# Expert rows added to the output by accumulating scatters instead of being stored and gathered

## The chip, the cores and the metric

The kernel runs on one core of a Trainium2 chip. The metric is the device time of one execution in microseconds. Three timed runs of the kernel before gave 521.59, 524.7 and 526.0 us, a median of 524.7 us. The execution that the profiler recorded took 525.11 us, and its span, from the first to the last instruction, is 523.0 us.

## The reference, cut to what matters

The program is one layer of a graph network: 625 nodes with 512 features, a two-layer relational graph convolution and a linear-attention block side by side, and then a feed-forward block with routed experts. Only the last block is touched. It computes, for each node row (the capacity never binds for 625 nodes):

```python
f = _layernorm(x)
y = gelu(f @ Ws1 + bs1) @ Ws2 + bs2                 # shared expert
for bank in ("sp", "fq"):                           # two banks of 8 experts
    probs = softmax(f @ Wr + br)
    expert = argmax(probs)                          # one expert a node and bank
    gate = probs[expert]
    h = gelu(f @ W1[expert] + b1[expert])           # 512 -> 128
    y += gate * (h @ W2[expert] + b2[expert])       # 128 -> 512
out = x + y
```

Each node takes one expert in each of two banks, so each output row is the node's residual row plus one shared term and two gated expert rows. With the inputs of this case the reference sends 1, 0, 226, 17, 321, 60, 0 and 0 nodes to the experts of the first bank, and 0, 0, 6, 31, 306, 20, 130 and 132 to those of the second.

## The kernel before, in words

Nodes are tiled as 5 blocks of 125 rows (`NT`, `TP`). A tile scheduler fixes each engine's order of instructions when the program is built, from the order in the source and from priorities. Where two tiles share a tag they share memory, and the later one waits until the earlier one is no longer read.

The end of the kernel, from line 1240 on, goes so:

- **Residual and normalised rows.** `x1` holds the residual of every node in SBUF, `fn` its layer norm. `fn` is stored to DRAM (`fn_d`, line 1245).
- **Routing.** VectorE (DVE) finds each node's expert in each bank, its place in the order sorted by expert (`place`), and the list of nodes in that order (`node_i`, lines 1284 to 1321).
- **Windows.** Each expert's nodes are cut into windows of 128 rows (`WIN`). `NW` = 12 windows a bank are always computed, since up to 12 can be needed. `offs` holds for every window the offset of its expert's weights and its first row (lines 1324 to 1350); TensorE and DVE load these as registers. `slot_i` says for each node in which of the 12 x 128 window rows its result stands (line 1360).
- **Shared expert.** Line 1382 computes it, with the gated expert biases (`mT`, `b2x`), two products a block, and line 1383 adds it to `x1` on DVE.
- **Sorted rows.** GpSimd (POOL) gathers `fn` rows in sorted order by indirect transfers (line 1400, 5 a bank), TensorE turns them (line 1408), and ACT and DVE copy them into `sortT`.
- **First expert layer**, a loop over the 12 windows (lines 1412 to 1419): DVE copies the window's weights to `stage1`, TensorE does 4 products, ACT applies Gelu into `hid`.
- **Second expert layer**, another loop over the 12 windows (lines 1420 to 1424): one product, a copy out of PSUM into one of 4 buffers of `stage` by ACT, or in the first bank by ACT and DVE in turn, and a store of 128 rows to DRAM (`back_d`) from SyncE's queue (SP).
- **Rows back to their nodes** (lines 1425 to 1433): for each block POOL gathers 125 rows of `back_d` by `slot_i`, DVE multiplies them by `gate` and adds them to `x1`, and after the second bank SP stores the block of the output. The gathers' buffer of the first bank has tag A, which is also the tag of `sort_fq`, the second bank's sorted rows.

The two banks go one after another on TensorE. PSUM buffers for the second layer (`narrow`) are two.

Of the kernel before, what the change touches and what calls it, by code (L numbers as in the profile page):

```python
# [40 lines left out]
EARLY = 2  # L41
WIN = 128
NW = (N + NX * (WIN - 1)) // WIN
WHOLE = 1.5 * 2 ** 23


# [542 lines left out]
def tile_fast(ctx: ExitStack, tc: tile.TileContext, a: dict, out: bass.AP, flag):  # L589
# [10 lines left out]
    def fourth(tag, name, shape=(TP, NT, H)):  # L600
        return main.tile(list(shape), F32, tag=tag, name=name)
# [167 lines left out]
    def nodes(t):  # L769
        return slice(t * TP, (t + 1) * TP)  # L770
# [426 lines left out]
    nc.gpsimd.tensor_copy(low_2, lower)  # L1197
    number = const.tile([TP, NT], F16, name="number")
    nc.gpsimd.iota(number, pattern=[[TP, NT]], base=0, channel_multiplier=1, allow_small_or_imprecise_dtypes=True)
    iota_w = const.tile([128, NW], F32, name="iota_w")  # L1200
    nc.gpsimd.iota(iota_w, pattern=[[1, NW]], base=0, channel_multiplier=0, allow_small_or_imprecise_dtypes=True)

# [67 lines left out]
        return ap[:, :, None].to_broadcast([TP, G, NX])  # L1270

    SW = KC * N + WIN
    room = main.tile([128, 2 * NT * H], F32, tag="U", name="room")
    sortT = [room[:, :SW], main.tile([128, SW], F32, tag="A", name="sort_fq")]
    halves = room[:TP, SW:].bitcast(F16)
# [121 lines left out]
    back_d = [dram.tile([NW * WIN, H], F32, name=f"back{i}") for i in range(2)]  # L1397
# [5 lines left out]
    for i in range(2):  # L1403
        sT = sortT[i][:, :KC * N].rearrange("p (k n) -> p k n", n=N)
        for t in range(NT):
            ps = wide_ps("ps_sT")[:, :KC * 128].rearrange("p (k n) -> p k n", n=128)
            for k in range(KC):
                nc.tensor.transpose(ps[:, k, :TP], rows_s[i][:, t, k * 128:(k + 1) * 128], ident[:TP, :TP])
            (nc.vector.tensor_copy if t % 2 else nc.scalar.copy)(sT[:, :, nodes(t)], ps[:, :, :TP])
        at = offsets(i, 0, (NX - 1) * H, [mybir.EngineType.PE, mybir.EngineType.DVE])  # L1410
        start = offsets(i, 1, N - 1, [mybir.EngineType.PE])
        for w in range(NW):
            w1s = stage1[:, w % 4, :]
            nc.vector.tensor_copy(w1s, we1[i][:, bass.ds(at[w], KC * FF)])
            ps = wide_ps("ps_hid")[:, :WIN]
            for k in range(KC):
                nc.tensor.matmul(ps, w1s[:, k * FF:(k + 1) * FF], sortT[i][:, k * N:][:, bass.ds(start[w], WIN)],
                                 start=(k == 0), stop=(k == KC - 1))
            nc.scalar.activation(hid[i][:, w * WIN:(w + 1) * WIN], ps, AF.Gelu, bias=bias[:, i, w:w + 1])
        for w in range(NW):  # L1420
            ps = narrow([(hid[i][:, w * WIN:(w + 1) * WIN], we2[i][:, bass.ds(at[w], H)])], m=WIN)
            y = stage[:, w % 4, :]
            (nc.vector.tensor_copy if w % 2 and not i else nc.scalar.copy)(y, ps)
            nc.sync.dma_start(back_d[i][w * WIN:(w + 1) * WIN, :], y)
        yg = fourth("AX"[i], f"got{i}")
        for t in range(NT):
            nc.gpsimd.indirect_dma_start(  # L1427
                yg[:, t, :], None, back_d[i][:, :],
                bass.IndirectOffsetOnAxis(ap=slot_i[:, 2 * t + i:2 * t + i + 1], axis=0))
            nc.vector.scalar_tensor_tensor(x1[:, t, :], yg[:, t, :], gate[:, 2 * t + i:2 * t + i + 1], x1[:, t, :],  # L1430
                                           op0=ALU.mult, op1=ALU.add)
            if i == 1:
                nc.sync.dma_start(out[nodes(t), :], x1[:, t, :])


@with_exitstack
# [42 lines left out]
```

## Time and profile before

| what | value |
|---|---|
| median of the runs shown | 524.7 us |
| profiled execution | 525.11 us |
| its span | 523.0 us |
| mean granted TensorE clock | 0.938 |
| PE, DVE, ACT, POOL busy share | 87%, 71%, 39%, 16% |
| first gather of sorted rows starts | 418.74 us |
| first expert layer, bank sp, starts | 437.94 us |
| second expert layer, bank sp, starts | 448.76 us |
| first expert layer, bank fq, starts | 464.81 us |
| second expert layer, bank fq, starts | 477.22 us |
| last product of all | 492.45 us |
| last vector instruction of all | 511.17 us |

The shares of busy time cover the whole span, and in the first 400 us TensorE is busy nearly throughout. The change lies in the last 100 us, so that the stretches of that part, and not the shares, are what is to be read. The profile names a transfer by what it writes and reads (`back<-stage`), and a bracket at the end of a timeline line gives the engine's idle time before it and what ended that idle time.

### The profile page before, as it was taken

How to read it: one execution, taken by the hardware profiler on the slowest of the kernel's cores; microseconds unless marked ns; L12 is line 12 of the kernel's file. 1: busy time of each engine (PE TensorE's matmuls, PEld its weight loads, DVE VectorE, ACT ScalarE, POOL GpSimd, SP SyncE). 2: the span in 40 equal slices, each digit the busy share in tenths (PEclk: the TensorE clock that was granted, in tenths of full speed). 3: DMA queues.
4: the chain of work that ended last, by engine and by line, in shares of the span. 5: the costliest groups of instructions: out<-in, count | busy, mean ns of one | idle time of the engine just before them, and what ended most of it. 6: DMA issues, size and time to landing. Idle time of an engine off the chain costs nothing. (4 is left out here: it accounts for less than half of the span.)

```text
span 523.0 us, 5583 instructions
## 1 busy us (share of the span) xinstructions
PE 456.6 (87%) x1945; PEld 278.9 (53%) x1945; DVE 369.1 (71%) x452; ACT 202.7 (39%) x339; POOL 83.6 (16%) x117
## 2 busy tenths in 40 slices
PE   0389999999999999999999999999998799989400
PEld 0255358677665545687444769644444556566100
DVE  2659979999989769999999889997313454241220
ACT  1653149998998553161000345200001412334300
POOL 5700000000002111000000001970001071003140
PEclk9999999999999689999999889999999869989955
DMA  8957785453446957985767954995501542322742
GB/s 210 376 161 245 245 276 192 127 196 102 141 142 213 260 155 230 313 295 161 226 228 245 326 161 127 301 319 140 191 28 25 176 124 74 141 102 74 268 108 93
DMA packets 55751, 98.31 MB, mean 188 GB/s; under 512 B 6006, under 2 KB 14322, under 8 KB 55716
## 3 DMA queue, kind: packets, MB, share of 16 engines
q1 hardware_dynamic: 47204, 80.25, 47.4%
q0 software_dynamic: 8512, 17.63, 11.9%
q8 instruction: 18, 0.29, 0.2%
q14 instruction: 17, 0.14, 0.1%
HBM read 89.00 MB, written 8.85 MB: 187 GB/s over the span
## 5 line engine op out<-in xcount | busy, mean ns | idle before, releaser
L822 DVE SCALAR_TENSOR_TENSOR wrel<-basis_sb,att,wrel 128x2048 f32<-128x2048 f32 x107 | 246.0, 2346 | 7.7 <-DMA basis_sb<-in_L_gnn_basis_dram 5.7
L964 ACT ACTIVATE side<-iota_h,ed_f 125x630 f16<-125x630 f16 x96 | 71.9, 814 | 2.0 <-PE ps_cnt L969 2.0
L969 PE MATMUL ps_cnt<-side,oh_source 125*125 125x315 f16 x192 | 39.3, 302 | 0.2 <-DVE oh_source L966 0.2
L969 PEld LDWEIGHTS <-oh_source 125*125 125x125 f16 x192 | 25.7, 138 | 23.5 <-issue 15.4
L1220 PE MATMUL ps_acc<-wrel,agg 128*125 128x512 f32 x80 | 36.5, 596 | 0.3 <-DVE v L1240 0.3
L766 PE MATMUL ps_narrow<-wrel,agg 128*125 128x512 f32 x80 | 35.0, 592 | 0.0
L966 DVE TENSOR_SCALAR oh_source<-iota_h,col_m,ed_f 125x128 f16<-125x128 f16 x96 | 25.1, 312 | 10.9 <-PE ps_cnt L969 10.8
L1430 DVE SCALAR_TENSOR_TENSOR v<-got,work,v 125x512 f32<-125x512 f32 x10 | 7.5, 752 | 30.1 <-DMA got<-back,slot_i 30.1
L1089 PE MATMUL ps_agg<-cnt,high 125*128 125x314 f32 x160 | 26.9, 311 | 1.1 <-ACT wrel L854 1.1
L1089 PE MATMUL ps_agg<-cnt,low 125*128 125x314 f32 x160 | 26.4, 308 | 0.0
L1089 PEld LDWEIGHTS ps_agg<-cnt,high 125*128 125x128 f32 x160 | 24.1, 189 | 2.5 <-ACT wrel L854 2.0
L766 PEld LDWEIGHTS ps_narrow<-wrel,agg 128*125 128x125 f32 x80 | 15.0, 188 | 18.8 <-issue 18.8
L1089 PEld LDWEIGHTS ps_agg<-cnt,low 125*128 125x128 f32 x160 | 24.0, 189 | 0.8 <-issue 0.8
L1220 PEld LDWEIGHTS ps_acc<-wrel,agg 128*125 128x125 f32 x80 | 14.6, 187 | 17.5 <-issue 16.5
L766 PE MATMUL ps_narrow<-root,xnT 128*125 128x512 f32 x40 | 23.8, 739 | 0.0
L1183 POOL TENSOR_SCALAR_AFFINE_SELECT work<-work 125x125 f16<-125x125 f16 x1 | 23.7, 23719 | 0.0
L1240 DVE TENSOR_TENSOR v<-v,ps_acc 125x512 f32<-125x512 f32 x5 | 3.4, 687 | 26.7 <-PE ps_acc L1220 26.7
L1427 POOL DMA_INDIRECT got<-back,slot_i x10 | 12.1, 1211 | 59.7 <-PE ps_narrow L766 44.5
L760 PE MATMUL ps_wide<-zT,wq 128*128 128x512 f32 (+1 forms) x64 | 20.7, 433 | 0.0
L1105 ACT ACTIVATE gpre<-ps_narrow 125x512 f32<-125x512 f32 x5 | 3.0, 597 | 45.3 <-PE ps_narrow L766 45.3
L1220 PE MATMUL ps_acc<-root,gT 128*125 128x512 f32 x40 | 20.5, 647 | 0.0
L713 ACT COPY agg<-ps_agg 128x628 f32<-128x628 f32 x16 | 10.8, 680 | 22.9 <-PE ps_agg L1089 22.9
(282 smaller groups left out, 730.2 us busy)
## 6 DMA issues: line engine op xcount, KB each, us to landing
basis_sb<-in_L_gnn_basis_dram SPq DMA_DIRECT2D x56, 1024.0 KB
back<-stage SPq DMA_DIRECT2D x24, 256.0 KB
quad<-in_L_gnn_basis_dram POOLq DMA_DIRECT2D x16, 256.0 KB, 6.9
w<-in_L_mix_W_dram POOLq DMA_DIRECT2D x2, 1024.0 KB
root<-in_L_gnn_root_dram POOLq DMA_DIRECT2D x2, 1024.0 KB, 7.9
we_sp<-in_L_ffn_W_sp_dram SPq DMA_DIRECT2D x4, 512.0 KB
we_fq<-in_L_ffn_W_fq_dram SPq DMA_DIRECT2D x4, 512.0 KB
we_sp<-in_L_ffn_W_sp_dram SPq DMA_DIRECT2D x2, 1024.0 KB
```

Source lines behind the costliest of these rows:

```text
L713: nc.scalar.copy(dst, src)
L760: nc.tensor.matmul(ps[:, lo:hi], s, m[:, lo:hi], start=(i == 0), stop=(i == len(pairs) - 1))
L766: nc.tensor.matmul(ps[:m, :n], s, mv, start=(i == 0), stop=(i == len(pairs) - 1))
L822: final = nc.vector.scalar_tensor_tensor(dst, src, s, dst, op0=ALU.mult, op1=ALU.add)
L964: later(lambda: nc.scalar.activation(side, iota_h[:EP], AF.Sign, bias=row_f[:, c:c + 1]))
L966: later(lambda: nc.vector.tensor_scalar(os, iota_h[:EP, :128], col_m[:, m, c:c + 1], code_f[:, c:c + 1], op0=ALU.is_equal, op1=ALU.mult))
L969: nc.tensor.matmul(ps[:TP, s, :SEG + 1], os[:, :TP], side[:, s * SEG:(s + 1) * SEG + 1], start=(c == STEPS[m][0]), stop=(c == STEPS[m][-1]))
L1089: nc.tensor.matmul(ps[:, s, :SEG], y, cnt[:, r, m, s * SEG:(s + 1) * SEG].bitcast(F32R), start=(i == 0), stop=(i == len(pairs) - 1))
L1183: nc.gpsimd.affine_select(before, before, compare_op=ALU.is_ge, fill=0.0, base=-1, pattern=[[1, TP]], channel_multiplier=-1)
L1220: nc.tensor.matmul(accs[t], s, mv, start=start and i == 0, stop=stop and i == len(pairs) - 1)
L1427: nc.gpsimd.indirect_dma_start(yg[:, t, :], None, back_d[i][:, :], bass.IndirectOffsetOnAxis(ap=slot_i[:, 2 * t + i:2 * t + i + 1], axis=0))
L1430: nc.vector.scalar_tensor_tensor(x1[:, t, :], yg[:, t, :], gate[:, 2 * t + i:2 * t + i + 1], x1[:, t, :], op0=ALU.mult, op1=ALU.add)
```

## The change

The result of a window is no longer stored to a scratch tensor and gathered back. Instead:

- the output is first stored without the experts, block by block, right after line 1383;
- each window's result is multiplied by its rows' gates while it is copied out of PSUM into `stage` (ACT for even windows, DVE for odd ones, in both banks);
- POOL then issues an indirect transfer per window that adds the 128 rows of `stage` to the rows of the output in DRAM named by a list, `node_s`; a list entry of a row that holds no node lies beyond the last row, and is left out by the bounds check. Within a bank the scatters are declared independent of one another;
- the lists and gates in window order (`node_s`, `gate_s`) are made by products with one-hot matrices: ten of 125 x 128 against 125 x 24, for which DVE makes the one-hot rows and copies out the results;
- the loops of the two expert layers are merged: the second layer of window w follows the first layer of window w + 2 (`LAG`).

Stores to `back_d` (24), gathers from it (10) and the additions of gathered rows (10) go away; 24 scatters come in. The number of output stores stays at 5.

```diff
+LAG = 2
@@
-    slot_i = const.tile([TP, G], I32, name="slot_i")
...
-    nc.vector.tensor_tensor(slot_i, place, slot, op=ALU.subtract)
+    nc.vector.tensor_tensor(slot, place, slot, op=ALU.subtract)
+    window = small_tile(TP, G)
+    nc.vector.tensor_scalar(window, slot, 1.0 / WIN, (0.5 - WIN / 2) / WIN, op0=ALU.mult, op1=ALU.add)
+    nc.vector.tensor_scalar(window, window, WHOLE, -WHOLE, op0=ALU.add, op1=ALU.add)
+    nc.vector.scalar_tensor_tensor(slot, window, -float(WIN), slot, op0=ALU.mult, op1=ALU.add)
@@
+    both = spare[:TP, :4 * NT * NW].rearrange("p (j t i w) -> p j t i w", j=2, t=NT, i=2)
+    eq = both[:, 1]
+    nc.vector.tensor_tensor(eq, iota_w[:TP, None, None, :].to_broadcast([TP, NT, 2, NW]),
+                            window.rearrange("p (t i) -> p t i", i=2)[:, :, :, None].to_broadcast([TP, NT, 2, NW]),
+                            op=ALU.is_equal)
+    nc.vector.tensor_tensor(both[:, 0], eq, number1[:, :, None, None].to_broadcast([TP, NT, 2, NW]), op=ALU.mult)
+    nc.vector.tensor_tensor(eq, eq, gate.rearrange("p (t i) -> p t i", i=2)[:, :, :, None]
+                            .to_broadcast([TP, NT, 2, NW]), op=ALU.mult)
+    gate_s = small_tile(WIN, 2, NW)
+    node_s = const.tile([WIN, 2, NW], I32, name="node_s")
+    for i in range(2):
+        ps = pn.tile([128, 512], F32, tag="narrow", name="ps_rows")
+        ps = ps[:, :2 * NW].rearrange("p (j w) -> p j w", j=2)
+        for t in range(NT):
+            oh = spare[:TP, 4 * NT * NW + (t % 2) * WIN:4 * NT * NW + (t % 2 + 1) * WIN]
+            nc.vector.tensor_scalar(oh, iota_r[:TP], slot[:, 2 * t + i:2 * t + i + 1], None, op0=ALU.is_equal)
+            nc.tensor.matmul(ps, oh, both[:, :, t, i, :], start=(t == 0), stop=(t == NT - 1))
+        nc.vector.tensor_copy(gate_s[:, i, :], ps[:, 1, :])
+        none = small_tile(WIN, NW)
+        nc.vector.tensor_scalar(none, ps[:, 0, :], 0.0, 2.0 * N, op0=ALU.is_equal, op1=ALU.mult)
+        nc.vector.scalar_tensor_tensor(node_s[:, i, :], ps[:, 0, :], -1.0, none, op0=ALU.add, op1=ALU.add)
@@
         nc.vector.tensor_tensor(x1[:, t, :], x1[:, t, :], ps, op=ALU.add)
+        nc.sync.dma_start(out[nodes(t), :], x1[:, t, :])
@@
-        for w in range(NW):
-            w1s = stage1[:, w % 4, :]
...
-        for w in range(NW):
-            ps = narrow([(hid[i][:, w * WIN:(w + 1) * WIN], we2[i][:, bass.ds(at[w], H)])], m=WIN)
-            y = stage[:, w % 4, :]
-            (nc.vector.tensor_copy if w % 2 and not i else nc.scalar.copy)(y, ps)
-            nc.sync.dma_start(back_d[i][w * WIN:(w + 1) * WIN, :], y)
-        yg = fourth("AX"[i], f"got{i}")
-        for t in range(NT):
-            nc.gpsimd.indirect_dma_start(
-                yg[:, t, :], None, back_d[i][:, :],
-                bass.IndirectOffsetOnAxis(ap=slot_i[:, 2 * t + i:2 * t + i + 1], axis=0))
-            nc.vector.scalar_tensor_tensor(x1[:, t, :], yg[:, t, :], gate[:, 2 * t + i:2 * t + i + 1], x1[:, t, :],
-                                           op0=ALU.mult, op1=ALU.add)
-            if i == 1:
-                nc.sync.dma_start(out[nodes(t), :], x1[:, t, :])
+        added = []
+        def second(w):
+            ps = narrow([(hid[i][:, w * WIN:(w + 1) * WIN], we2[i][:, bass.ds(at[w], H)])], m=WIN)
+            y = stage[:, w % 4, :]
+            s = gate_s[:, i, w:w + 1]
+            if w % 2:
+                nc.vector.tensor_scalar(y, ps, s, None, op0=ALU.mult)
+            else:
+                nc.scalar.activation(y, ps, AF.Copy, scale=s)
+            add = nc.gpsimd.indirect_dma_start(
+                out[:, :], bass.IndirectOffsetOnAxis(ap=node_s[:, i, w:w + 1], axis=0), y, None,
+                bounds_check=N - 1, oob_is_err=False, compute_op=ALU.add)
+            if added:
+                tc.declare_no_dep(add.ins, group=f"rows{i}", reason="each node has one row in a bank's windows")
+            tc.add_to_no_dep_group(f"rows{i}", add.ins)
+            added.append(w)
+        for w in range(NW + LAG):
+            if w < NW:
+                w1s = stage1[:, w % 4, :]
...
+            if w >= LAG:
+                second(w - LAG)
```

More of the change, by code (lines that the diff above doesn't have):

```diff
@@ L1199, in tile_fast @@
     nc.gpsimd.iota(number, pattern=[[TP, NT]], base=0, channel_multiplier=1, allow_small_or_imprecise_dtypes=True)
+    number1 = const.tile([TP, NT], F32, name="number1")
+    nc.gpsimd.iota(number1, pattern=[[TP, NT]], base=1, channel_multiplier=1, allow_small_or_imprecise_dtypes=True)
+    iota_r = small_tile(128, WIN)
+    nc.gpsimd.iota(iota_r, pattern=[[1, WIN]], base=0, channel_multiplier=0, allow_small_or_imprecise_dtypes=True)
     iota_w = const.tile([128, NW], F32, name="iota_w")
@@ L1272, in tile_fast @@
     SW = KC * N + WIN
-    room = main.tile([128, 2 * NT * H], F32, tag="U", name="room")
+    room = main.tile([128, 2 * NT * H + 16], F32, tag="U", name="room")
+    spare = room[:, SW + (6 * N + 258) // 2:]
     sortT = [room[:, :SW], main.tile([128, SW], F32, tag="A", name="sort_fq")]
-    halves = room[:TP, SW:].bitcast(F16)
+    halves = room[:TP, SW:SW + (6 * N + 258) // 2].bitcast(F16)
     iota_n = halves[:, :N]
@@ L1395, in offsets @@
             skip_runtime_bounds_check_because="capped when they are made")[1]
-    back_d = [dram.tile([NW * WIN, H], F32, name=f"back{i}") for i in range(2)]
     for i in range(2):
@@ L1411, in tile_fast @@
         start = offsets(i, 1, N - 1, [mybir.EngineType.PE])
-        for w in range(NW):
-            w1s = stage1[:, w % 4, :]
[L1414 to L1419, printed above, removed]
@@ new lines, in tile_fast @@
+        for w in range(NW + LAG):
+            if w < NW:
+                w1s = stage1[:, w % 4, :]
+                nc.vector.tensor_copy(w1s, we1[i][:, bass.ds(at[w], KC * FF)])
+                ps = wide_ps("ps_hid")[:, :WIN]
+                for k in range(KC):
+                    nc.tensor.matmul(ps, w1s[:, k * FF:(k + 1) * FF], sortT[i][:, k * N:][:, bass.ds(start[w], WIN)],
+                                     start=(k == 0), stop=(k == KC - 1))
+                nc.scalar.activation(hid[i][:, w * WIN:(w + 1) * WIN], ps, AF.Gelu, bias=bias[:, i, w:w + 1])
+            if w >= LAG:
+                second(w - LAG)
```

## The prediction

> **What bounds the kernel now.** I read first the chain that ended last, since the change lies at the end; it reaches back only to 502.58 us, so I then read the timeline of the last 100 us, and the transfers in short stretches.
>
> In the timeline, POOL's first gather of window results starts at 478.33 us, as the second bank's first layer leaves its sorted rows. Its second set starts only when the last window is stored, at 498.39 us. From there nothing runs but five gathers, five additions and five stores:
>
> ```profile
> 477.22 6.43 PE L766 MATMUL ps_narrow<-we_fq 128*128 x14
> ...
> 478.33 1.21 POOL L1427 DMA_INDIRECT got<-back,slot_i  x1 [44.50 <-PE ps_narrow L766]
> ...
> 485.46 0.75 DVE L1430 SCALAR_TENSOR_TENSOR v<-got,work,v 125x512 f32<-125x512 f32 x1 [11.18 <-DMA got<-back,slot_i]
> ...
> 493.61 0.59 ACT L1423 COPY stage<-ps_narrow 128x512 f32<-128x512 f32 x1 [0.59 <-PE ps_narrow L766]
> 498.39 1.21 POOL L1427 DMA_INDIRECT got<-back,slot_i  x1 [12.80 <-DMA back<-stage]
> ...
> 504.46 1.21 POOL L1427 DMA_INDIRECT got<-back,slot_i  x1 [0.30 <-issue]
> 504.65 0.75 DVE L1430 SCALAR_TENSOR_TENSOR v<-got,work,v 125x512 f32<-125x512 f32 x1 [12.67 <-DMA got<-back,slot_i]
> 505.43 6.78 SPq L1433 DMA_DIRECT2D out_dram<-v  x5
> ...
> 511.17 0.75 DVE L1430 SCALAR_TENSOR_TENSOR v<-got,work,v 125x512 f32<-125x512 f32 x1 [1.53 <-DMA got<-back,slot_i]
> ```
>
> The columns of the next view are stretch, length, busy time of PE, PEld, DVE, ACT and POOL, granted clock, share of the 16 DMA engines, GB/s:
>
> ```profile
> 508.50:518.50 10.00, 0.00 (x0) 0.00 (x0) 1.50 (x2) 0.00 (x0) 0.00 (x0) 0.50 0.33 127
> 518.50:520.50 2.00, 0.00 (x0) 0.00 (x0) 0.00 (x0) 0.00 (x0) 0.00 (x0) 0.50 0.18 72
> 520.50:523.00 2.50, 0.00 (x0) 0.00 (x0) 0.00 (x0) 0.00 (x0) 0.00 (x0) 0.50 0.00 0
> ```
>
> The five output stores (1.28 MB) run at 127 GB/s, a third of the engines, until about 520; then 2.5 us of ending. So for the 29 us after the last product, which ends at 493.6, all computing engines are nearly idle.
>
> **What goes.** The 24 stores, 10 gathers and 10 additions. With them go the wait for the last store, 5 x 1.51 us of POOL, the last landing (504.46 to 511.10), and 10 us of output stores from the end. What is late next is the first scatter.
>
> **When the first scatter can start.** It waits for all five output stores, and these for the shared expert. In the changed program as built TensorE no longer does part of the shared products while it waits for rows: all five pairs stand behind the turning of the sorted rows, among the first two windows.
>
> ```profile
> 433.35 1.12 PE L766 MATMUL ps_narrow<-ws,hsh 128*125 128x512 f32 x2
> ...
> 434.41 1.12 PE L766 MATMUL ps_narrow<-b2x,mT 17*125 17x512 f32 x2
> ...
> 437.94 10.98 PE L1417 MATMUL ps_hid<-room,stage 128*128 x96
> ...
> 448.76 11.43 PE L766 MATMUL ps_narrow<-we_sp 128*128 x24
> ```
>
> A pair takes 2.1 us (433.35 to 435.45), a window's first layer 0.9 us (10.98/12), its second 0.95 us. The last gather of sp's rows is issued at 425.04; from issue to use the first ones took 7.1 us, so 432.1. Then on TensorE: turning 0.65, ten one-hot products at about 0.3 (an estimate between 0.13, router product 128x16, and 0.41, turning 125x125) 3.0, the register load 0.76, two windows 1.8, five pairs 10.6: 449.0. DVE's new work, 22 small instructions of 0.17 to 0.35 us (rows of its neighbours of like shape), some 5 us in all, lies partly in its 4.06 us of idle time before 428.06 and otherwise beside TensorE's 17 us; without that cover it would add up to 5. The last addition takes 0.69 and its store starts at 449.7. The store of 256 KB issued after 493.61+0.59 was seen landed at 498.39, 4.2 us, of which 0.9 is its bytes at the 284 GB/s of 480 to 490 us; with 2.0 for 256 KB at 127 GB/s, 5.3. **First scatter: 455 us** (451 to 458). By then four windows stand ready.
>
> **The rate of scatters.** Three things bound it.
>
> 1. POOL: a gather takes 1.21 with 0.30 between, so 1.51 a scatter.
> 2. TensorE: 0.9 + 0.95 = 1.85 a window, 7.4 for four.
> 3. The four buffers of `stage`: the copy of window w waits until scatter w-4 has landed. ACT and DVE do Gelu, weight copies and these copies in order, and TensorE has two PSUM buffers, so everything behind a waiting copy stands too. Four windows therefore take the time L from a scatter's issue to its landing, plus 0.8 for copy and semaphores.
>
> L isn't in the trace: no transfer there adds. Nearest rows: the ten gathers took 5.7 to 7.4 us from issue to the waiting addition, 6.6 on average. From below: SP's store of 128 rows, 4.2, and 0.9 more for POOL's longer issue, 5.1. From above: a read of the rows and then a write, one after the other, 7.1 + 4.2 = 11.3. I take 6.6, as the queue and the kind of transfer are the same. Against a gather speaks the addition; for it, that 128 rows may use more engines than 125, and that only 625 of 1536 window rows hold a node (8 of 12 windows of the first bank, 10 of the second by the counts above), so that the last scatters of each bank carry next to nothing.
>
> The output stores' share of 0.33 at 127 GB/s is five engines of sixteen. [...]
>
> **The sum.** A bank takes 2 groups of max(7.4, L + 0.8), then 3 x 1.51 = 4.5 and L. The second bank's first scatter waits for all of the first's. With L = 6.6: 14.8 + 4.5 + 6.6 = 25.9 a bank; 455 + 51.8 + 2.5 = 509.3 us of span, and 2.1 (525.11 - 523.0) around it: **511 us**. The profiled execution lies 0.4 above the median, within the scatter of the runs, so it stands for the median. For L from 6 to 8 and the first scatter 451 to 458 it is 506 to 520.
>
> **The rivals.**
>
> - *Scatters land like plain stores* (L = 5.1). TensorE sets the rate: 24.4 a bank, 508. For it: rows that hold no node; against: POOL's gathers never did.
> - *Reading, adding and writing one after the other*, **slower**. L = 11.3, groups of 12.1, 40 a bank: 455 + 80 + 4.6 = 540. It decides from L = 8.9, where the sum is the 525 of before; around there lie the outcomes within 1%. [...]
> [...]
> - *The change doesn't do what it says*: every scatter waits for the one before, 24 x 7.4 us, 635. The built program shows no such waits within a bank.
>
> **How the numbers follow.** My forecast 0.50, store-like 0.15, L near 9 0.09, read-then-write 0.13, POOL 0.11, serial 0.02. So faster by over 1% 0.65, within 1% (about what the runs, 521.6 to 526.0, can tell from no change) 0.09, slower 0.26. The forecast's own range is 506 to 520; with the store-like case's low end and POOL's 535 the range is 503 to 536, which leaves out the read-then-write case, the serial one and little below.
>
> **What would show it.** First scatter at 451 to 458; POOL's time for one near 1.2; waits of ACT and DVE on scatters of four windows earlier, in groups of about 7.4; one long wait of POOL between the banks, equal to L; the end 2 to 3 us after the last landing, with no output stores near it. An L over 8.9 or a POOL time over 2 makes the prediction wrong; so would output stores that land well after 455.

## The result and the profile after

Fourteen runs of the changed kernel have a median of 516.48 us (506.71 to 523.51), fourteen of the kernel before on the same chip 524.61 us (520.88 to 527.55). The ratio is **0.975, 95% interval 0.970 to 0.980**: faster. This ratio, and the others below, leave out runs that lie over 1.5% above a kernel's fastest, which here leaves the four at the higher mean clock (0.946 and up); over all runs the medians give 0.984. The predicted time was 511, the range 503 to 536.

The spread is itself a result. In the changed kernel's runs time follows the mean granted clock of TensorE: four runs at 0.946 to 0.958 took 506.7 to 513.0, ten at 0.924 to 0.937 took 514.8 to 523.5. A line through these 14 and four later runs is 910.5 - 421.5 x clock, with 1.4 us left over: **0.01 of mean clock is 4.2 us**. Below, "at the same clock" is the mean distance from this line. The mean clock also counts stretches in which TensorE has nothing to do (the last 14.5 us of the kernel before stand at 0.50), so the line serves to compare the changed kernel with its variants, and not with the kernel before.

The profiled execution (516.71 us, span 515.0, clock 0.929) is one of the ten at the lower clock. The timeline of its tail, from answers for TensorE, VectorE, SP's queue and POOL; the columns are start, us, engine, line, operation, and in brackets the idle time before with what ended it:

```profile
452.11 2.06 PE L767 MATMUL ps_narrow<-b2x,mT 17*125 17x512 f32 x2
...
454.21 0.69 DVE L1417 TENSOR_TENSOR v<-v,ps_narrow 125x512 f32<-125x512 f32 x1 [3.30 <-PE ps_narrow L767]
...
436.82 18.38 SPq L1418 DMA_DIRECT2D out_dram<-v  x5
...
460.16 1.63 POOL L1458 DMA_INDIRECT out_dram<-stage,node_s  x1 [31.20 <-SPq L1486]
...
489.28 1.61 POOL L1458 DMA_INDIRECT out_dram<-stage,node_s  x1 [6.92 <-ACT stage L1457]
...
510.34 1.55 POOL L1458 DMA_INDIRECT out_dram<-stage,node_s  x1 [0.30 <-DMA out_dram<-stage,node_s]
```

One shared product (a row with x2, since it is recorded as two) took 2.06 us where the rows of the prediction have 1.12, so a pair of them 4.0 us instead of 2.1. The last addition ended at 454.9, its store was issued right behind it, and the first scatter starts at 460.16, 5.2 us behind that issue; the wait ahead of it is put down to SP's queue, which issues these stores. The first bank's last scatter is issued at 480.81. POOL then idles 6.92 us, released by ACT's copy of the second bank's first window (488.13 to 488.82 in ACT's timeline), not by landings. The last scatter is issued at 510.34, and the span ends 4.7 us later, with no output stores near.

The products were slow because of the clock. The columns are stretch, length, busy time of PE, PEld, DVE, ACT and POOL, granted clock, share of the 16 DMA engines, GB/s:

```profile
405.00:410.00 5.00, 2.63 (x22) 1.99 (x20) 3.88 (x17) 3.95 (x6) 0.00 (x0) 0.76 0.30 117
410.00:430.00 20.00, 16.69 (x95) 14.17 (x96) 11.37 (x50) 2.40 (x4) 12.73 (x10) 0.50 0.42 111
430.00:455.00 25.00, 25.00 (x46) 10.36 (x46) 5.40 (x13) 0.73 (x2) 0.00 (x0) 0.50 0.18 57
455.00:460.00 5.00, 5.00 (x19) 3.49 (x19) 1.12 (x3) 1.42 (x3) 0.00 (x0) 0.62 0.17 53
```

The clock fell at 407.6 and came back at 458.8, though TensorE was busy all the time from 430 on. In the profile of before it fell at 413.6 and was back at 427.2. There the first shared products ran at the half clock too, in rows ahead of those that the prediction read:

```profile
421.90 2.05 PE L766 MATMUL ps_narrow<-ws,hsh 128*125 128x512 f32 x2
```

The prediction took the price of the last three pairs, at the full clock, for all five.

The page's group of the scatters, and their line among the DMA issues (columns of the group: count, busy us, mean ns of one, idle us before and what ended it; of the issues: count, median us from issue to landing):

```profile
L1458 POOL DMA_INDIRECT out_dram<-stage,node_s x24 | 37.7, 1571 | 45.2 <-SPq L1486 31.2
...
out_dram<-stage,node_s POOLq DMA_INDIRECT x24, 4.4
```

A scatter holds POOL for 1.55 us (median; 1.57 on average), a gather 1.21. With 0.30 between two of them a scatter takes 1.85, and that is the interval nearly everywhere: 20.65 us for the eleven intervals of the first bank, 21.06 for the second's. A scatter lands 4.4 us after its issue.

### The profile page after: what moved, and what is told of

It reads as the page before. It is cut to its first block, busy times and chain, and to the rows that moved or that the text cites. A ratio compares the mean times of both kernels' runs of the same rounds, so it can differ in the third digit from the quotient of the medians.

```text
span 515.0 us, 5629 instructions
## 1 busy us (share of the span) xinstructions
PE 468.6 (91%) x1965; PEld 288.9 (56%) x1965; DVE 370.3 (72%) x470; ACT 200.4 (39%) x333; POOL 109.8 (21%) x133
## 4 chain that ended last, share of the span: by engine, by line
PE 68%; DMA 12%; DVE 10%; issue 6%; POOL 3%; ACT 1%; DVEq 0%; POOLq 0%; ACTq 0%
PE ps_narrow L767 26%; PE ps_acc L1225 15%; PE ps_wide L761 7%; PE ps_agg L1090 7%; DVE wrel L823 6%; PE ps_hid L1472 4%; PE ps_cnt L970 4%; DMA out_dram<-stage,node_s 3%; DMA basis_sb<-in_L_gnn_basis_dram 2%; PE ps_gate L779 2%; DMA we_fq<-in_L_ffn_W_fq_dram 1%; DMA att<-in_L_gnn_att_dram 1%; PE ps_flip L750 1%; DMA wr<-in_L_ffn_Wr_sp_dram 1%; DVE oh_source L967 1%
## 5 line engine op out<-in xcount | busy, mean ns | idle before, releaser
L1458 POOL DMA_INDIRECT out_dram<-stage,node_s x24 | 37.7, 1571 | 45.2 <-SPq L1486 31.2
L1225 PEld LDWEIGHTS ps_acc<-wrel,agg 128*125 128x125 f32 x80 | 14.5, 187 | 17.6 <-issue 16.5
L1225 PE MATMUL ps_acc<-root,gT 128*125 128x512 f32 x40 | 20.4, 643 | 0.0
L1455 DVE TENSOR_SCALAR stage<-ps_narrow,work 128x512 f32<-128x512 f32 x12 | 9.0, 751 | 15.5 <-DMA out_dram<-stage,node_s 11.5
L1472 PEld LDWEIGHTS ps_hid<-room,stage 128*128 128x128 f32 x96 | 16.0, 238 | 6.5 <-issue 6.4
```

The lines of the kernel that those rows point to most:

```text
L1225: nc.tensor.matmul(accs[t], s, mv, start=start and i == 0, stop=stop and i == len(pairs) - 1)
L1458: add = nc.gpsimd.indirect_dma_start(out[:, :], bass.IndirectOffsetOnAxis(ap=node_s[:, i, w:w + 1], axis=0), y, None, bounds_check=N - 1, ...
```

## The experiments

The theory after this profile: (1) the half clock, which begins at TensorE's waits behind the router and lasts through those for the sorted rows, makes the late first scatter and the spread; (2) from then on POOL's 1.85 us per scatter paces the end. The rivals: the spread comes from the scatters; landings, four windows on, pace the end; the gain is not the scattering's at all. Each profile below is one execution; where its first gather of sorted rows starts varies from 413.4 to 419.0 us from run to run, with nothing changed ahead of it, so the first scatter is counted from there. All times in us, from the timelines of POOL; "gap" is from the last scatter of the first bank to the first of the second:

| kernel | first gather | first scatter behind it | first bank, 11 intervals | gap | second bank, 11 intervals | clock 0.5 from, to |
|---|---|---|---|---|---|---|
| changed, first profile | 413.49 | 46.67 | 20.65 | 8.47 | 21.06 | 407.6, 458.8 |
| changed, second profile | 418.62 | 36.73 | 20.67 | 6.34 | 20.66 | 414.2, 438.1 |
| lists_late | 416.07 | 39.85 | 20.83 | 6.28 | 20.89 | 411.5, 452.5 |
| late_warm | 418.43 | 38.56 | 20.91 | 5.94 | 20.65 | 416.5, 426.8 and 433.6, 454.1 |
| lag12 | 415.72 | 41.08 | 20.47 | 16.31 | 20.43 | 411.1, 435.0 |
| no_add | 419.02 | 46.41 | 17.18 | 6.95 | 18.98 | 412.8, 464.0 |
| stage8 | 416.78 | 37.24 | 20.62 | 4.38 | 20.43 | 412.2, 436.1 |
| best2 | 416.02 | 36.35 | 20.72 | 4.38 | 20.43 | 411.5, 435.4 |
| best | 415.90 | 29.62 | 22.27 | 4.39 | 20.42 | 411.5, 431.9 |
| wide_node | 415.80 | 34.26 | 22.70 | 4.40 | 20.43 | 425.5, 446.0 |

The edges of the clock are read from stretches of 1 us. These show 1.00 or 0.50 in all profiles, and a value between only at an edge: where one shows 0.76, the clock was full for 0.52 of it.

### The changed kernel again

No edit.

> The changed kernel as it is, as the base for the runs beside it. If the half clock behind the gathered rows makes its spread (theory 1), runs with a mean granted clock near 0.956 take 506 to 509 us and runs near 0.927 take 516 to 523, and a profile at the higher clock shows the first scatter some 8 to 12 us earlier than 460.16, with the same 1.85 us from scatter to scatter behind it. If the spread comes from the scatters themselves (theory 2), a profile at the higher clock shows the first scatter near 460 and shorter intervals or landings behind it.

Four runs: 507.0 and 509.4 at clocks 0.958 and 0.948, 517.2 and 520.6 at 0.932 and 0.927. This profile fell at the higher clock (509.38 us, span 507.7). POOL's timeline of it:

```profile
418.62 1.42 POOL L1434 DMA_INDIRECT rows_sp<-fn_d,node_i  x1 [13.68 <-DVE room L1321]
...
455.35 1.73 POOL L1458 DMA_INDIRECT out_dram<-stage,node_s  x1 [21.30 <-ACT stage L1457]
...
476.02 1.55 POOL L1458 DMA_INDIRECT out_dram<-stage,node_s  x1 [0.30 <-issue]
482.36 1.61 POOL L1458 DMA_INDIRECT out_dram<-stage,node_s  x1 [4.79 <-ACT stage L1457]
...
503.02 1.55 POOL L1458 DMA_INDIRECT out_dram<-stage,node_s  x1 [0.30 <-DMA out_dram<-stage,node_s]
```

And its stretches around the return of the clock:

```profile
430.00:435.00 5.00, 4.99 (x25) 4.87 (x25) 2.34 (x10) 0.62 (x2) 3.44 (x3) 0.50 0.58 166
435.00:440.00 5.00, 5.00 (x19) 3.18 (x19) 1.52 (x5) 0.33 (x1) 0.00 (x0) 0.69 0.20 75
440.00:445.00 5.00, 5.00 (x18) 1.96 (x17) 1.77 (x6) 0.37 (x1) 0.00 (x0) 1.00 0.21 63
```

The half clock was 24 us long instead of 51, and the first scatter came 9.9 us earlier behind the first gather. Theory 1 holds for the spread: the scatters' own part, 20.67 and 20.66, is the same to 0.4 us in both profiles. The bracket of the first scatter names another engine here, ACT with its copies (21.30 <-ACT). But ACT's copy of window 0 ended at 451.44, 3.9 us before the scatter:

```profile
450.75 0.69 ACT L1457 ACTIVATE stage<-ps_narrow,work 128x512 f32<-128x512 f32 x1 [0.49 <-PE ps_narrow L767]
```

The last output store was issued at 450.0, 5.4 us before the scatter, as it was 5.2 before it in the first profile. So here, too, its landing is what the scatter waited for last.

### The lists made behind the shared products

```diff
-    both = spare[:TP, :4 * NT * NW].rearrange("p (j t i w) -> p j t i w", j=2, t=NT, i=2)
-    ...
-        nc.vector.scalar_tensor_tensor(node_s[:, i, :], ps[:, 0, :], -1.0, none, op0=ALU.add, op1=ALU.add)
     hsh = yp.tile([FF, N], F32, tag="y", name="hsh", bufs=4)
     ...
         nc.sync.dma_start(out[nodes(t), :], x1[:, t, :])
+    both = spare[:TP, :4 * NT * NW].rearrange("p (j t i w) -> p j t i w", j=2, t=NT, i=2)
+    ...
+        nc.vector.scalar_tensor_tensor(node_s[:, i, :], ps[:, 0, :], -1.0, none, op0=ALU.add, op1=ALU.add)
```

The block itself is unchanged.

> The block that makes the lists of rows and of gate values stands behind the shared expert's products in the source, so these no longer wait for the two narrow PSUM buffers that the lists hold, and fill TensorE's waits for the sorted rows as they do in the kernel before. Theory 1 (the shared products behind the lists leave TensorE idle, and the half clock then doubles their time): clock back at 1.0 by about 430, last output store issued by about 440, first scatter at 445 to 450 instead of 460.16, time 497 to 506 us in all runs, spread under 1%. Theory 2 (the clock falls whatever stands there, or POOL's pace sets the end whatever the start): clock at 0.5 until about 458 again and time as the changed kernel's, 506 to 523.

Four runs, 505.99 to 512.59, median 509.55, ratio 0.974 (0.965 to 0.983). At the same clock they lie 4.2 us under the changed kernel, and the four runs spread by 6.6 us, where four of the changed kernel beside them spread by 13.6. But the clock stayed at 0.5 until 452.5, and the first scatter came no earlier than in the second profile above. It also waited for something else: the last output store was issued earlier, at 445.9, and the scatter starts 0.3 us behind ACT's copy of window 0 (454.94 to 455.63), which now stands behind the lists. So the first theory is half right: by these four runs, shared products that fill the waits are worth about 4 us, and they do not bring the clock back. That part of it falls.

### Products that only keep TensorE busy

On top of lists_late:

```diff
+    def fill(n):
+        for _ in range(n):
+            nc.tensor.matmul(ps_sh[:TP, 640:], every[:, :TP], iota_n[:, :384], start=True, stop=True)
+
+    fill(6)
     ps = pn.tile([128, 512], F32, tag="narrow", name="ps_load")
     ...
+    fill(8)
     node_i = const.tile([TP, 2, NT], I32, name="node_i")
```

> As lists_late, with 14 half-precision products of 125x125 by 384 columns, whose result nobody reads, put where TensorE waits between the router's result and the sorting (where the granted clock falls in every trace so far). If the half clock behind that point makes the late first scatter and the spread (theory 1, second form): the clock stays at 1.0 or comes back within 5 us, the first scatter starts 27 to 32 us behind the first gather of sorted rows (40 in lists_late, 37 to 47 in the changed kernel), the mean granted clock rises from 0.935-0.948 to over 0.96, and the runs take 496 to 502 us within 4 us of each other. If the clock falls for another reason than these waits: 0.5 for 20 to 50 us again, and 506 to 513 us as lists_late.

Median 510.63 (508.98 to 514.69), ratio 0.980 (0.974 to 0.987): no gain over lists_late. The added products run in the waits as meant, and the clock holds through them; it falls afterwards, among the products that sort the node numbers, which have one column each. TensorE's timeline:

```profile
414.78 3.12 PE L1331 MATMUL ps_node<-number,room 125*125 125x1 f16 x25
...
433.78 2.04 PE L767 MATMUL ps_narrow<-ws,hsh 128*125 128x512 f32 x2 [3.19 <-issue]
```

And the stretches:

```profile
411.00:416.00 5.00, 4.70 (x34) 3.11 (x32) 3.78 (x17) 2.49 (x4) 0.00 (x0) 1.00 0.21 85
416.00:417.00 1.00, 1.00 (x14) 1.00 (x15) 0.59 (x2) 0.00 (x0) 0.00 (x0) 0.76 0.08 16
417.00:422.00 5.00, 4.40 (x37) 4.04 (x36) 2.24 (x10) 0.00 (x0) 2.96 (x3) 0.50 0.10 24
```

It came back at 426.8, fell again at 433.6, at the end of a wait of 3.19 us, and stayed low for 20.5 us, nearly all of them dense products. So the fall has its place, at waits and at one-column products, as far as one profile tells; what ends the half clock is not shown by these runs.

### The second layer not following closely

```diff
-LAG = 2
+LAG = NW
```

> The second layer starts after all twelve first layers of its bank (LAG = NW), everything else as changed. If following closely is what brings the second bank's scatters forward, its first scatter comes ten windows of first layer later, 10 x 0.9 = 9 us behind the second bank's first product; the first bank loses nothing, since its scatters wait for the output stores anyway: 9 us more than the changed kernel. If the scatters' pace alone sets the end and first layers lie beside it, under 2 us.

Median 527.06 (520.2 to 536.64, ten runs); ratio to the kernel before 1.001 (0.994 to 1.008), and 8.6 us over the changed kernel at the same clock: 9 were expected. Over all runs beside it the medians give 1.009. The scatters themselves are as quick as ever; the second bank's first one waits for twelve first layers. POOL's timeline:

```profile
477.27 1.55 POOL L1458 DMA_INDIRECT out_dram<-stage,node_s  x1 [0.30 <-issue]
493.58 1.57 POOL L1458 DMA_INDIRECT out_dram<-stage,node_s  x1 [14.76 <-ACT stage L1457]
```

14.76 us of idle time against 4.79 in the second profile of the changed kernel, 10.0 us more. **Scattering without following closely wins nothing.**

### The scatter without its addition

```diff
-                bounds_check=N - 1, oob_is_err=False, compute_op=ALU.add)
+                bounds_check=N - 1, oob_is_err=False)
```

> The same scatters without the addition (they overwrite, so the output lacks the residual, the shared expert and a part of the other bank). If the addition is what makes POOL take 1.55 us for a scatter where it took 1.21 for a gather, POOL's time falls to 1.21 and the interval to TensorE's 1.85 or less, with landings of 4 to 5 us instead of 4.4 to 7.7, and 2 to 5 us of the time go. If it is the bounds check or the 128 rows, POOL stays at 1.55, the interval at 1.85, and the time within 1 us; if only landings are longer by the addition, POOL stays at 1.55 and the waits of ACT and DVE for free buffers, 20.4 us now, fall by half or more.

Four runs, 498.4 to 514.81, ratio 0.959 (0.948 to 0.971); 7.9 us under the changed kernel at the same clock. The scatters' group in the lines view, and their line among the DMA issues:

```profile
L1458 POOL DMA_INDIRECT out_dram<-stage,node_s x24 | 25.6, 1068 | 49.5 <-SPq L1486 31.0 <-ACT stage L1457 10.3 <-DVE stage L1455 5.8
...
out_dram<-stage,node_s POOLq DMA_INDIRECT x24, 2.7
```

POOL's time falls from 1.57 to 1.07 us on average (0.98 to 1.21), and the landing from 4.4 or 4.7 to 2.7 us. The bounds check and the 128 rows are still there, so it is the addition that costs POOL the half microsecond. The interval falls to 1.56 in the first bank and 1.73 in the second, on average. Where copies stand ready it is 1.3, which is POOL's own time; elsewhere POOL waits for ACT's and DVE's copies in turn, and the intervals alternate between 1.69 and 1.81: 1.75 is the pace of TensorE and the copies without POOL in the way. 24 x (1.85 - 1.65) = 4.8 us of the 7.9 are so accounted for; the rest is open.

### Eight buffers for the copies

```diff
-    stage = main.tile([WIN, 4, H], F32, tag="w8", name="stage", bufs=3)
+    stage = [main.tile([WIN, 4, H], F32, tag="w8", name=f"stage{j}", bufs=3) for j in range(2)]
...
-            y = stage[:, w % 4, :]
+            y = stage[w // 4 % 2][:, w % 4, :]
```

> The changed kernel with eight buffers for the copies of window results instead of four. If the landing of a scatter, four windows on, sets the rate (the ring as the prediction had it), the intervals between scatters fall below 1.85 us and the time by 5 us or more. If POOL sets it (1.55 and 0.30 between), the interval stays 1.85 in both banks; ACT's and DVE's 20 us of waits on scatters go, and only the gap of POOL between the banks shrinks, from 4.8 to 6.9 us to 0.3 to 3: 2 to 5 us less than the changed kernel at the same granted clock.

Median 512.25 (505.81 to 517.36), ratio 0.973 (0.965 to 0.982), 3.4 us under the changed kernel at the same clock. DVE's copies in the lines view of the changed kernel's second profile:

```profile
L1455 DVE TENSOR_SCALAR stage<-ps_narrow,work 128x512 f32<-128x512 f32 x12 | 9.0, 750 | 18.3 <-DMA out_dram<-stage,node_s 12.7 <-PE ps_narrow L767 5.5
```

The same group of stage8, its POOL timeline around the gap, ACT's copy of the second bank's first window, and a wait of POOL's queue (duration in ns, then its start):

```profile
L1455 DVE TENSOR_SCALAR stage<-ps_narrow,work 128x512 f32<-128x512 f32 x12 | 9.0, 751 | 11.1 <-PE ps_narrow L767 11.1
...
474.64 1.55 POOL L1458 DMA_INDIRECT out_dram<-stage,node_s  x1 [0.30 <-issue]
479.02 1.57 POOL L1458 DMA_INDIRECT out_dram<-stage,node_s  x1 [2.83 <-ACT we_fq L1474]
...
474.24 0.69 ACT L1457 ACTIVATE stage<-ps_narrow,work 128x512 f32<-128x512 f32 x1 [0.49 <-PE ps_narrow L767]
...
L1458 POOLq EVENT_SEMAPHORE  x1: 7126/7126/7126, 470.2 to 470.2; - x1
```

The waits of DVE and ACT for landings, 25.9 us in the changed kernel's second profile (12.7 and 13.2), are gone to the last tenth, and the interval has not moved: 20.62 and 20.43 for eleven. So the landings stood beside POOL's time and did not pace the scatters. What they did delay is the second bank's first copy: the gap between the banks fell from 6.34 to 4.38 us. These 2.0 us are part of the 3.4; the rest is not accounted for.

The gap that is left is a wait for a landing. The copy that the scatter of 479.02 needs ended at 474.93, 4.1 us earlier, and the Gelu that the bracket names is one of a later window. POOL's queue waits until 477.4, 2.7 us behind the issue of the first bank's last scatter at 474.64, and 2.7 is what that scatter took to land in the changed kernel's two profiles. From there 1.7 us pass to the next scatter.

### Parts of the gain on the kernel before

The kernel before with its output stores cut in two:

```diff
-                nc.sync.dma_start(out[nodes(t), :], x1[:, t, :])
+                for lo, hi in ((0, 112), (112, TP)):
+                    nc.sync.dma_start(out[t * TP + lo:t * TP + hi, :], x1[lo:hi, t, :])
```

> The kernel before, with each output store of 125 rows cut into 112 and 13 rows and nothing else. If the old tail is set by stores that use five of sixteen DMA engines, the stores behind the last addition land about 4 us after it instead of 8: 3 to 5 us less than the kernel before, and a part of what the change won is had without it. If the tail is set by the gathers and additions alone, under 1 us.

The kernel before with the second layer two windows behind the first, and copies by ACT and DVE in both banks:

```diff
-        for w in range(NW):
-            w1s = stage1[:, w % 4, :]
+        for w in range(NW + 2):
+            if w < NW:
+                w1s = stage1[:, w % 4, :]
...
-        for w in range(NW):
-            ps = narrow([(hid[i][:, w * WIN:(w + 1) * WIN], we2[i][:, bass.ds(at[w], H)])], m=WIN)
+            if w >= 2:
+                second(w - 2)
```

`second` holds the product, the copy (DVE for odd windows, ACT for even ones) and the store.

> The kernel before, with its second layer following the first by two windows, copies shared by ACT and DVE in both banks, rows stored and gathered as before: one half of the change alone. The gathers wait for a bank's last window whatever the order, and TensorE has the same work up to it, so theory: within 2 us of the kernel before. Rival: the stores spread over the first layer's time and land earlier, so that both gathers start 3 to 6 us earlier.

And the two together:

> The kernel before with both of its small edits, second layer two windows behind the first and output stores cut into 112 and 13 rows; rows are still stored and gathered. Each alone gave 0.991. If they take different stretches (the last window's store; the output stores behind the last addition), they add up to 0.982, 511 to 514 us, about what the scattering kernel takes; then the scattering itself is worth under 1%. If they take the same stretch, 0.990.

before_split 516.09 us, ratio 0.991 (0.984 to 0.998); before_merged 516.78, 0.991 (0.984 to 0.998); before_both 514.99, 0.989 (0.983 to 0.996). A stretch in the tail of before_split with output stores alone, the gathers having landed by 512.6:

```profile
514.00:515.00 1.00, 0.00 (x0) 0.00 (x0) 0.00 (x0) 0.00 (x0) 0.00 (x0) 0.50 0.78 229
```

POOL's timeline of before_merged, the first and the second set of gathers:

```profile
480.13 1.21 POOL L1431 DMA_INDIRECT got<-back,slot_i  x1 [51.62 <-PE ps_narrow L766]
...
489.23 1.21 POOL L1431 DMA_INDIRECT got<-back,slot_i  x1 [1.83 <-DMA back<-stage]
```

With 112 and 13 rows the output stores run at 229 GB/s instead of 127, and the span ends 5.2 us behind the last addition instead of 11.1. The share of the 16 DMA engines is 0.78, not 0.33. It is a mean, and which engines were busy is not shown: "five of sixteen" is an estimate, 0.33 x 16 = 5.3. In before_merged the second set of gathers starts 75.8 us behind the first gather of sorted rows (413.39), where in before it was 79.7 (418.74 to 498.39): 3.8 us earlier, as the rival had it; "within 2 us" was wrong. TensorE no longer waits for ACT's copies there (in before it waited for them from 485.9 on, 0.2 to 2.3 us at a time), which fits, but the sharing of copies and the order were not tried apart. The two do not add up: that would have been 0.982, and they reach 0.989, as if they took the same stretch. So small edits of the old tail give 1.1%, the change 2.5% by its four runs at the higher clock and 1.6% over all of its runs.

### What the readings point to

The changed kernel with eight buffers, output stores of 112 and 13 rows, and the second bank's rows turned among the first bank's windows:

```diff
+            if not i and 5 <= w < 5 + NT:
+                turn_sorted(1, w - 5)
```

> The changed kernel with eight buffers for copies, the second bank's rows turned among the first bank's windows 5 to 9, and output stores cut into 112 and 13 rows. If POOL's 1.85 us from scatter to scatter paces the end, the gap between the banks (4.8 to 6.9 us; 2.8 with eight buffers) falls to under 1.5 and the first scatter comes 1 us earlier: 24 scatters take 44 to 46 us from the first to the last issue, and the time is 3 to 6 us below the changed kernel at the same granted clock (501 to 505 near 0.955, 511 to 516 near 0.927). If landings pace it, no more than stage8 gave.

And with the lists behind the shared products as well:

> As best2, and the lists of rows made behind the shared expert's products as in lists_late. lists_late kept the runs to 506.0 to 512.6 where the changed kernel spread from 506.7 to 523.5; if that is because its products fill TensorE's waits for rows, best takes 500 to 507 in all runs, 2% or more under the kernel before with a smaller spread than best2. If the narrow spread was chance, best spreads as best2 does, some 10 us.

best2: 504.3, 512.7, 514.7 and 514.7 at clocks 0.954, 0.930, 0.923 and 0.923, which is 5.8 us under the changed kernel at the same clock; the gap between the banks stayed at 4.38, where under 1.5 was expected, and it is the same as with eight buffers alone. The expectation left out the landing of the first bank's last scatter: the second bank's first copy was ready 4.6 us before its scatter (472.87 and 477.47), so turning the rows earlier could not shorten the gap. **best: 498.73 us (498.48 to 502.57), ratio 0.959 (0.953 to 0.965).** It beats both kernels. All four of its runs had clocks of 0.951 to 0.963 and lie within 4.1 us, those of best2 within 10.4, and its profile has the earliest first scatter of all, 29.6 us behind the first gather. POOL's timeline of it:

```profile
415.90 1.42 POOL L1435 DMA_INDIRECT rows_sp<-fn_d,node_i  x1 [13.67 <-DVE room L1321]
...
445.52 1.63 POOL L1462 DMA_INDIRECT out_dram<-stage,node_s  x1 [14.46 <-ACT stage L1461]
...
472.18 1.57 POOL L1462 DMA_INDIRECT out_dram<-stage,node_s  x1 [2.84 <-ACT we_fq L1478]
...
492.60 1.55 POOL L1462 DMA_INDIRECT out_dram<-stage,node_s  x1 [0.30 <-DMA out_dram<-stage,node_s]
```

The turning among the windows has its price: the first bank's eleven intervals take 22.27 us, with waits of 0.4 to 0.7 for the copies, and the gap is 4.39 as in best2, with the copy ready 2.8 us before the scatter.

### Wider products for the sort

```diff
-                nc.tensor.matmul(ps[:TP, s:s + 1], perm[:, t, nodes(s)], number[:, t:t + 1],
+                nc.tensor.matmul(ps[:TP, s * 64:(s + 1) * 64], perm[:, t, nodes(s)],
+                                 number[:, t:t + 1].to_broadcast([TP, 64]),
...
```

with the added products of late_warm, all on top of best.

> The kernel best with the 14 idle products of late_warm, and with the fifty products that sort the node numbers taking 64 equal columns instead of one (one of the 64 is read). In late_warm the clock stayed at 1.0 through the waits and fell at 416.8, in the middle of the one-column products, although TensorE shows as busy there. If a product of one column is too little work to hold the clock: it stays at 1.0 until at least 424, by when the shared products run, the first scatter starts 22 to 28 us behind the first gather (29.6 in best), mean granted clock 0.965 or more, time 490 to 497 us. If the clock follows something else: it falls before 420 again, for 10 to 50 us, and the time is that of best, 498 to 503, or 1 to 2 us over it for the wider products.

Four runs, 503.23 to 507.42, ratio 0.968 (0.958 to 0.979): 5 us slower than best. Its stretches:

```profile
416.00:421.00 5.00, 4.90 (x31) 2.38 (x30) 4.53 (x22) 0.67 (x1) 4.08 (x4) 1.00 0.29 74
421.00:425.00 4.00, 2.42 (x11) 1.12 (x10) 2.78 (x10) 0.58 (x1) 3.23 (x3) 1.00 0.78 193
425.00:426.00 1.00, 0.64 (x4) 0.57 (x4) 0.40 (x2) 0.00 (x0) 0.86 (x1) 0.77 0.78 251
426.00:429.00 3.00, 1.58 (x7) 0.94 (x6) 1.08 (x4) 0.58 (x1) 2.39 (x3) 0.50 0.85 241
429.00:445.00 16.00, 16.00 (x33) 6.97 (x33) 3.82 (x8) 0.95 (x2) 1.70 (x2) 0.50 0.36 109
```

The first half of the expectation came true: with 64 columns in place of one the same fifty products hold the clock, and it stays at 1.0 to 425.5. Then TensorE waits 1.81 us for gathered rows, until 425.36, and it falls there; a wait of 1.35 us follows, with only transposes between. The second half failed: the half clock again lasted 20.5 us, though TensorE was busy without a break from 429, and now it lay over the shared products and the lists instead of over the sort. Moving the fall later cost time. The time expected with it, 490 to 497 us, was missed by 6 us and more.

## Why the prediction was right, and where it was not, point by point

**What bounds the kernel, and what goes.** Right: nothing of the old tail is left; the last scatter is issued 4.7 us before the end of the span.

**First scatter at 455 us (451 to 458).** 460.16 in the first profile, whose first gather was 5.25 us early, so 10.4 late by its own steps; 455.35 in the second, whose first gather (418.62) is that of before (418.74). The step that failed is "a pair takes 2.1 us". That figure, and all of TensorE's in the sum, were read where the clock was back at 1.0; nothing in the sum carried the clock. At the half clock a pair takes 4.0, and the five pairs of the first profile cost 9.5 us more. In the second profile four of the five ran at the full clock, and the scatter came where the sum had it. Of the other terms, the ten list products took 4.6 us at the half clock and 4.1 in the second profile, against 3.0; the last store 5.2 and 5.4 from issue to the scatter, against 5.3, and its landing was the last wait, as the prediction had it. "By then four windows stand ready" was wrong: TensorE does the second layers behind the shared products, and when the first scatter started one copy was done in the first profile and three in the second.

**The rate.** The sum had 7.4 us for four windows, and 7.4 us it was, but by another engine. The prediction gave it to TensorE (1.85 a window) and POOL 1.51. POOL takes 1.55 + 0.30 = 1.85, and TensorE and the copies without it run at 1.75. The mis-sized term is "a gather takes 1.21", carried over to a scatter: 1.55 when it adds. That two engines came to the same 1.85 was luck.

**Landings and the ring of four.** L was set at 6.6 (5.1 to 11.3). Measured: 4.4 and 4.7 us in the median, 2.7 to 6.7 in the first profile, so below the low end. On 128 rows against 125 the kernel before shows stores only: those of 128 rows (452 to 460 us) had 0.71 to 0.75 of the engines at 262 to 279 GB/s, those of 125 rows 0.33 at 127; of scatters no run compares the two. The waits on scatters of four windows earlier are there, as said they would be, but they follow from POOL's pace and set none: stage8. Their one cost is in the gap between the banks, 2.0 us.

**Between the banks.** "One long wait of POOL between the banks, equal to L" was wrong in its cause for the changed kernel. POOL waits 4.79 to 6.92 us, and for the second bank's first copy: in the second profile the first bank's last scatter, issued at 476.02, lands 2.7 us later, and the copy ends at 481.91. With eight buffers the copy comes earlier, and then the wait is the predicted one: the gap is 4.38 to 4.40 in stage8, best2, best and wide_node, although the copy was ready 2.8 to 4.6 us before. It is 2.7 of landing and 1.7 of POOL, not 6.6. From first scatter to first scatter it took 27.0 us in the second profile (29.1 in the first), where the sum had 25.9, and behind the last issue 4.7 us where the sum had 6.6 + 2.5 = 9.1. With the first scatter at 455.35 this gives 455.35 + 27.0 + 20.66 + 4.68 = 507.7: 1.6 under the 509.3 of the sum, two errors of opposite sign.

**The rivals.** Scatters that land like plain stores (508) are nearest to the second profile, both in the time and in L. POOL as the bound, in the chances with 0.11 and in the range with 535, was right in kind: POOL does pace the scatters, at 1.85 us. No run shows the 2.72 a scatter that the 535 was worked out from; in its place the runs show 1.57 us of POOL with the addition and 1.07 without. The times of *reading, adding and writing one after the other* and *the change doesn't do what it says* did not come either: a landing takes 4.4 and 4.7 us in the median, not 11.3, and the next scatter starts after 1.85, not 7.4.

**The time.** 511, with medians of 516.5 and, four later runs, 513.3. By the terms of the sum, L = 8 and a first scatter at 458 give 523, not the 520 that the forecast's own range has as its end, and the store-like case's low end is 504, not 503. The runs at the higher clock lie at 507 to 513, those at the lower at 515 to 524; the difference is the half clock, for which the sum had no term.

**Where the gain comes from.** Four kernels of these runs make a square: neither part 1.000, following closely alone 0.991 (with the copies shared), scattering alone 1.001, both 0.975 (over all runs the last two are 1.009 and 0.984). Scatters occupy POOL for 20.4 us a bank, more than five gathers did; they pay because following closely puts that time beside the first layers.

## What to carry to other kernels

A transfer that takes the place of a store, a gather and an addition is to be priced by the time that it holds its issuing engine, its addition included (here 1.57 us of POOL, 1.07 without the addition), and by whether that time lies beside other work: neither half of this change was worth what both were (following closely alone 0.991, scattering alone 1.001, both 0.975). One shared product took 1.12 us at a granted clock of 1.00 and 2.06 at 0.50, so read the clock beside each row of TensorE's and give it a term of the sum where the work moves to a stretch in which TensorE waits. Waits that vanish without moving the interval, as those for the ring did (25.9 us of them, the interval 1.85 as before), were a shadow of the engine that sets the pace. And a releaser that a view names is to be held against the end of its own work: twice here ACT was named when the copy in question had been done for about 4 us, and the wait was for a transfer.

## What the runs showed of the hardware that was not expected

An adding scatter is dear in its transfer, too. At about the same bytes per second the DMA engines are about three times as busy as with the plain scatter. Two stretches of the changed kernel's second profile:

```profile
460.00:465.00 5.00, 3.96 (x24) 2.72 (x22) 1.51 (x3) 0.79 (x2) 4.09 (x4) 1.00 0.66 90
465.00:470.00 5.00, 4.11 (x17) 2.02 (x15) 1.76 (x4) 1.72 (x5) 4.39 (x3) 1.00 0.96 115
```

And two of no_add:

```profile
465.00:470.00 5.00, 5.00 (x30) 3.62 (x29) 2.78 (x5) 1.79 (x4) 3.50 (x4) 1.00 0.22 84
470.00:475.00 5.00, 5.00 (x31) 3.75 (x30) 1.96 (x4) 2.46 (x5) 3.14 (x4) 1.00 0.27 103
```

115 GB/s take 0.96 of the engines with the addition, 103 GB/s take 0.27 without.

The half clock came in steps. Its fifteen stays that began between 405 and 440 us, one in each of the fourteen profiles and two in late_warm, lasted 10.2 (once), 13.6 or 13.7 (three times), 20.5 (four), 23.9 (four), 41.0 (once) and 51.2 us (twice): 3, 4, 6, 7, 12 and 15 times 3.41, within 0.1 us. The 3.41 us is an estimate from these lengths (51.2 / 15). Stays of that length occur alone: in the first profile the clock fell at 482.7 and was back at 486.1, with TensorE busy for all of 483 to 486. But TensorE was also busy without a break for 25 us of the first profile (430 to 455) and for 16 us of wide_node's (429 to 445) while the clock stayed at half, so work without a break did not end it at the next step. Without added products the clock fell in every profile 7.1 to 4.4 us ahead of the first gather; in the three whose TensorE timelines were read there (before, the first of the changed kernel, best) this is where TensorE waits for 1.22 and 1.10 us behind the router. Products of one column did not hold it in late_warm, where it fell among them at 416.5, and products of 64 columns did in wide_node, where it stayed at 1.0 to 425.5. What decides after how many steps it comes back stays open: no run here settles it, and between mean clocks of 0.929 and 0.958 it is worth 12 us to the changed kernel, by the line through its runs.
